# Cross-attention on one core: query weights B11 kept on chip, values loaded by single quads, two copies aside

## The chip, the core and the metric

The kernel runs on one core of a Trainium2 chip. The core has five engines with queues of their own: TensorE (PE, with its weight loads, PEld, shown apart), VectorE (DVE), ScalarE (ACT), GpSimd (POOL) and SyncE (SP), which here issues nearly all DMA transfers. The metric is the device time of one execution in microseconds; lower is better.

## What is computed

Everything is float32. `x` is 8 batches of 256 rows of 1024; `ctx` has the same shape and serves as keys and as values; there are 32 heads of 32 columns.

```python
x = (hidden - mu) * rsqrt(var + 1e-5) * ln_gamma + ln_beta
Q, K, V = split_heads(x @ Wq.T), split_heads(ctx), split_heads(ctx)
scores = einsum('bhsd,bhtd->bhst', Q, K) * 32 ** -0.5
probs = softmax(where(mask, scores, -inf))
attn = einsum('bhst,bhtd->bhsd', probs, V)   # heads joined again
return hidden + attn @ Wout.T
```

## The kernel before

The work is cut into 64 quads of four heads (128 columns): quad n is batch n // 8, column block n % 8. The main loop (L903) has 64 slots, and slot n works on several quads at once: scores of quad n+1 (L479), softmax of quad n+1, values of quad n-2 (L622), a share of the output product of the batch before (L694), and a share of the queries for a later batch. Every engine runs its instructions in the order in which this loop writes them; the schedule is written out by hand, and engines meet through semaphores.

**Softmax and the moves behind it** (softmax_parts, L491). DVE takes the row minimum (L515; queries are made with a negative scale), ACT the exponential (L519), DVE the reciprocal of the sum (L526), POOL the scaling (L528), DVE the transpose in blocks of 32 into `pT` (L534, four per quad). Half of `pT` then lies on the wrong partitions. ACT copies this half aside into `pc` (L540, two copies per quad). SP then issues two moves pT<-pT (L600), then the loads that the slot has in a list `between`, then two moves pT<-pc (L604), which overwrite what the first two moves have read and so wait for their landing. Another list, `ahead`, is issued before the first moves. In slots 0 to 6 and 56 to 61 this tail of a quad is put off to the next slot, behind its first exponentials. `pc` lies in the pool `asp` with three buffers, `pT` in one with three.

**Values** (load_v, L140). One transfer of 512 KB loads the values of two quads, in `between` of every second slot; the pool `vp` has two such buffers.

**Queries.** For batches 0 to 2 the product is made with the whole weights (make_q, L331). From batch 3 on a batch is made with seven products of half size (a Strassen-like scheme) in the order of Q_PRODUCTS, one per slot, from slot 8(b-1)+2 on: 18, 26, 34, 42 and 50 (query_product, L432). Seven weight tiles of 8 KB a partition are needed: four quarters (B11, B12, B21, B22) and sums T1 to T4, which POOL makes in slots 9 to 22 (sum_wq, L385). The tile `wq` holds four of the seven; T3 and then T2 take the place of B12, and T4 that of B11. T1, B11 and T3 are stored to DRAM (keep_wq, L393) and pass in turn through the tile `ring` in each batch (load_ring, L405, halves of 512 KB): T1 three and two slots before the first product, B11 both halves in the slot of the first product, T3 both halves two slots later. The products that read the ring are S1 (first), A11 (third) and S3 (fifth).

**The start.** Slots 0 to 7 also load the output weights `wo` in eight transfers of 512 KB (L173), the last of them in slot 7, and move blocks of the next batch's x (xnT<-xe, L327). The first output product (A11, then A12, of batch 0) begins in slot 9 in the PSUM bank `po` that the second query product of slot 8 has used; ACT empties it in copy_q (L349). ACT's order at that point is: copy pc<-pT of quad 9, the query copies, second copy pc<-pT.

Of the kernel before, what the change touches and what calls it, by code (L numbers as in the profile page):

```python
# [46 lines left out]
F32 = mybir.dt.float32  # L47
# [4 lines left out]
P = 128  # L52
# [7 lines left out]
def xattn_kernel(  # L60
# [12 lines left out]
    B, S, D = x.shape  # L73
    T = mask.shape[2]
    HD = D // HEADS
# [6 lines left out]
    K = 32  # L82
    NA = P // K
    NI = T // (2 * K)
    assert NH == 4 and NS == 2 and NT == 2 and S == 256 and T == 256 and NA == 4
    NEG_SCALE = -1.0 / math.sqrt(HD)
    N = B * NQ

    const = ctx.enter_context(tc.tile_pool(name="const", bufs=1))
# [4 lines left out]
    vp = ctx.enter_context(tc.tile_pool(name="vp", bufs=2))  # L94
    atp = ctx.enter_context(tc.tile_pool(name="atp", bufs=3))
    ep = ctx.enter_context(tc.tile_pool(name="ep", bufs=4))
    ptp = ctx.enter_context(tc.tile_pool(name="ptp", bufs=3))
    asp = ctx.enter_context(tc.tile_pool(name="asp", bufs=3))
    up = ctx.enter_context(tc.tile_pool(name="up", bufs=1))
    sm = ctx.enter_context(tc.tile_pool(name="sm", bufs=8))  # L100
    dram = ctx.enter_context(tc.tile_pool(name="dram", bufs=1, space=bass.MemoryType.DRAM))
# [6 lines left out]
    NK = D // P // 2  # L108
    ring = const.tile([P, NK, NK, P], F32, tag="ring", name="ring")
# [13 lines left out]
    xs, ks, vs, rs = {}, {}, {}, {}  # L123
# [8 lines left out]
    def load_k(n):  # L132

        b, g = divmod(n, NQ)
        ks[n] = kp.tile([P, 2, T], F32, tag="k", name=f"k_{n}")
        nc.sync.dma_start(
            ks[n], kv[b, g // 2, :, : 2 * T].rearrange("p (g t) -> p g t", g=2)
        )

    def load_v(n):  # L140

        b, g = divmod(n, NQ)
        vs[n] = vp.tile([P, NI, 2 * P], F32, tag="v", name=f"v_{n}")
        nc.sync.dma_start(
            vs[n], kv[b, g // 2, :, 2 * T :].rearrange("p (i v) -> p i v", i=NI)
        )

    def load_res(b, s, h):
# [8 lines left out]
    sums_x = const.tile([P, 2, NK, NA, K], F32, tag="sx", name="sx")  # L157
    kept = {
        name: dram.tile([P, NK, NK * P], F32, tag=name, name=f"kept_{name}")
        for name in ("T1", "B11", "T3")  # L160
    }
    wo = const.tile([P, 7, NK, 512], F32, tag="wo", name="wo")
    B11, B21, B22, T1, T2, T3, T4 = range(7)
    B12 = T1

    def load_wq(o):
        nc.sync.dma_start(wq[:, o], wq_[o])
# [36 lines left out]
    for o in range(2, 5):  # L204
        load_wq(o)
    load_k(2)
    load_v(0)
    for o in range(5, 8):
        load_wq(o)

# [148 lines left out]
    def fold(o):  # L359
# [13 lines left out]
    SPLIT = 3  # L373
    SOON, LATE = 0, NK
    W_AT = {"B12": (SOON, 0), "B22": (SOON, NK), "B11": (LATE, 0), "B21": (LATE, NK),
            "T2": (SOON, 0), "T3": (SOON, 0), "T4": (LATE, 0)}

    def weights(name, o):

        if name == "ring":  # L380
            return ring[:, o]
        first, k = W_AT[name]
        return wq[:, first + o, ds(k, NK)]

    def sum_wq(to, o):  # L385

        to, a, b, op = {
            "T1": ("ring", "B12", "B11", ALU.subtract), "T3": ("T3", "B22", "B12", ALU.subtract),
            "T2": ("T2", "T3", "B11", ALU.add), "T4": ("T4", "B21", "T2", ALU.subtract),
        }[to]  # L390
        nc.gpsimd.tensor_tensor(weights(to, o), weights(a, o), weights(b, o), op)
# [13 lines left out]
    def load_ring(name, half):  # L405
# [1 line left out]
        nc.sync.dma_start(ring[:, pair].rearrange("p o c q -> p o (c q)"), kept[name][:, pair])  # L407

    Q_PRODUCTS = (
        ("S1", "ring", True), ("S4", "B22", False), ("A11", "ring", True), ("S2", "T2", False),  # L410
        ("S3", "ring", False), ("A22", "T4", False), ("A12", "B21", True),
    )

# [18 lines left out]
    def query_product(b, p):  # L432
        name, which, begins = Q_PRODUCTS[p]
        if begins:
            pqs[b] = ps_q.tile([P, NK, P], F32, tag="pq", name=f"pq_{b}_{name}")
        x_ = x_part(b, name)
        for o in range(NK):
            w = weights(which, o)
            for c in range(NK):
                nc.tensor.matmul(  # L440
                    pqs[b][:, o, :], w[:, c], x_[:, c], start=begins and o + c == 0,
                    stop=c == NK - 1, skip_group_check=True,
                )
# [40 lines left out]
    def softmax(*args):  # L484
        for _ in softmax_parts(*args):
            pass
# [127 lines left out]
    def values(n):  # L614
        pvs[n] = [
            ps_v.tile([P, 2, NS, K], F32, tag="pv", name=f"pv_{n}_{r}") for r in range(2)
        ]
        pT = pTs.pop(n)
        for i in range(NI):
            for j in range(NH):  # L620
                for r in range(2):
                    nc.tensor.matmul(  # L622
                        pvs[n][r][j * HD : (j + 1) * HD],
                        vs[n - n % 2][ts(r, 2 * K), i, ds(n % 2 * P + j * HD, HD)],
                        pT[ts(r, 2 * K), :, i, j, :, :],
                        start=(i == 0), stop=(i == NI - 1),
                    )

    def copy_at(n):
        b, c = divmod(n, NQ)  # L630
        k, c = divmod(c, NK)
        if c == 0:
            ats[b, k] = atp.tile([P, NK, NS, NA, K], F32, tag="at", name=f"at_{b}_{k}")
        for r, pv in enumerate(pvs.pop(n)):
            nc.scalar.copy(  # L635
                ats[b, k][:, c, :, ts(r, 2), :], pv.rearrange("p a s k -> p s a k")
            )
# [144 lines left out]
    firsts = {NQ * (b - 1) + 2: b for b in range(SPLIT, B)}  # L782
# [55 lines left out]

    away, rings = {n: [] for n in range(N)}, {n: [] for n in range(N)}
    for n, name, half in (  # L840
        (9, "B11", 0), (10, "B11", 1), (15, "T1", 0), (16, "T1", 1), (17, "T3", 0), (19, "T3", 1),
    ):
        away[n].append(partial(keep_wq, name, half))
    for n, b in firsts.items():
        for slots, name in (((n - 3, n - 2), "T1"), ((n, n), "B11"), ((n + 2, n + 2), "T3")):
            if b > SPLIT or name != "T1":
                for half, slot in enumerate(slots):
                    rings[slot].append(partial(load_ring, name, half))
# [35 lines left out]
    for b in range(B - 1):  # L884
        done, ends = 0, b == B - 2
        for i, counts in enumerate(ENDS if ends else STEPS):
            n = NQ * (b + 1) + i
# [15 lines left out]
    for n in range(N):  # L903
        b, i = divmod(n - NQ, NQ)
        new_q = new_qs[n]
        between = []
        if n % 2 and n + 1 < N:
            between.append(partial(load_v, n + 1))
        elif n % 2 == 0 and n + 4 < N:
            between.append(partial(load_k, n + 4))  # L910
        ahead = rings[n]
        if n + 3 in firsts or n + 2 in firsts:
            between, ahead = between + ahead, []
        if b >= 0:
            if b == B - 2 and i - 1 in (5, 6):
                between.append(partial(send, b, *ENDS_TO[i - 1]))
# [24 lines left out]
        if n >= 2:  # L941
            values(n - 2)
# [20 lines left out]
        if n + 1 < N:  # L963
            softmax(n + 1, copies, ahead, between, hooks, fill)
        else:
            copy_at(n - 2)
            for load in between:
                load()
        if b >= 0 and i == 1:
            sum_at(b, "S2", *((slice(NK - 1, NK),) if b == B - 2 else ()))  # L970
# [68 lines left out]
    for c in range(2):  # L1039
        end_steps(to_c11, "A12", B21, (c,), (0,))  # L1040
        end_steps(to_c21, "A22", T4, (c,), (0,))
    values(N - 2)
    copy_at(N - 2)
    end_sum(slice(2, 3), nc.gpsimd)
# [3 lines left out]
    s2t2 = ps_o.tile([P, 512], F32, tag="po", name="po_end_s2")  # L1048
    end_steps(s2t2, "S2", T2, range(2), (0,))
    values(N - 1)  # L1050
    copy_at(N - 1)
    end_sum(slice(3, 4), nc.vector)
# [66 lines left out]
```

## Time and profile before

| what | us |
|---|---|
| median of three runs | 575.7 (574.19 to 576.84) |
| span of the profiled execution, first to last instruction | 577.6 |
| PE busy | 567.7 (98%) |
| DVE, ACT, POOL busy | 458.6, 412.1, 404.7 |
| values, v<-in_kv: 32 transfers of 512 KB, median to landing | 4.2 |
| keys, k<-in_kv: 32 of 256 KB | 3.0 |
| ring: 18 of 512 KB from T1 and T3, 10 from B11 | 5.8 and 5.9 |
| pT<-pT and pT<-pc: 128 each, 128 KB | 2.9 and 4.7 |

In all 117.98 MB were moved by the transfers, at 204 GB/s on average. No time of the profiled execution is given beside its span, so the span stands for it; it is 1.9 us above the median of the timed runs.

How to read the lines further on. A line of the timeline gives start, length, engine, source line, operation, output<-input, and in square brackets the idle time before it with what ended it. "issue" is waiting for which the profile shows no cause. SPq and PEld are the queues of SP and of PE's weight loads. Each float32 matmul of the program stands as two matmuls in the trace. A line of stages gives the stretch, its length, and then for PE, PEld, DVE, ACT and POOL the busy time with the number of instructions; then PE's granted clock, the busy share of the DMA engines and GB/s.

### The profile page before, as it was taken

Reading aid. Unit: us, or ns where it says so; the run is one execution under the profiler, and the core shown is the slowest. Engines: PE = TensorE matmul, PEld = TensorE weight load, DVE = VectorE, ACT = ScalarE, POOL = GpSimd, SP = SyncE. Lnnn points to the kernel's source line nnn. Section 1 sums busy time; section 2 is a strip of 40 time slices with the busy share of each in tenths; the row PEclk is TensorE's granted clock in tenths of the full one; section 3 lists DMA queues with packets and bytes.
Section 4 is the critical chain, followed back from the end, with each engine's and each line's share of the span. In section 5 each row is a group of like instructions: output and inputs, shape, how many; then the busy total and the mean of one; then the engine's idle time right before and its main releaser. Section 6 shows DMA issues by size and latency. Waiting matters only on the chain.

```text
span 577.6 us, 20001 instructions
## 1 busy us (share of the span) xinstructions
PE 567.7 (98%) x7162; PEld 392.2 (68%) x7162; DVE 458.6 (79%) x1695; ACT 412.1 (71%) x1425; POOL 404.7 (70%) x672
## 2 busy tenths in 40 slices
PE   8999998999999999899999999999999999999998
PEld 8788884666667777477776677667766777755444
DVE  6897887687878878678888888888877868879823
ACT  4688886677758857678577976779767866869820
POOL 1788998699896896665657775676656667448780
PEclk9999999999999999999999999999999999999999
DMA  8675778756778667776686767887658865436741
GB/s 312 224 211 184 218 240 209 244 172 196 196 229 271 215 188 219 225 222 202 181 247 181 233 196 201 237 257 217 186 160 254 239 192 147 130 112 182 214 154 74
DMA packets 47475, 117.98 MB, mean 204 GB/s; under 512 B 9104, under 2 KB 9872, under 8 KB 47376
## 3 DMA queue, kind: packets, MB, share of 16 engines
q1 hardware_dynamic: 47088, 116.69, 68.2%
q8 instruction: 57, 0.93, 0.7%
q14 instruction: 42, 0.34, 0.2%
q10 hardware_dynamic: 288, 0.01, 0.0%
HBM read 65.28 MB, written 11.53 MB: 133 GB/s over the span
## 4 chain that ended last, share of the span: by engine, by line
PE 79%; POOL 8%; DVE 6%; issue 2%; DMA 2%; ACT 1%; SPq 0%; DVEq 0%; POOLq 0%; ACTq 0%
PE po_S L694 17%; PE pq_A L440 16%; PE sc L479 10%; PE po_A L694 10%; PE pv L622 9%; PE pq_S L440 6%; POOL e L528 6%; PE pq L340 6%; DVE e L515 3%; PE po_end L761 2%; DVE pT L534 1%; PE po_last L761 1%; POOL wo L183 1%; DMA pT<-pT 1%; ACT e L519 1%
## 5 line engine op out<-in xcount | busy, mean ns | idle before, releaser
L528 POOL TENSOR_SCALAR e<-e,rden 128x256 f32<-128x256 f32 x512 | 237.0, 483 | 131.1 <-DVE rden L526 129.6
L519 ACT ACTIVATE e<-e,mn 128x256 f32<-128x256 f32 x512 | 254.0, 500 | 53.8 <-DVE mn L515 53.8
L534 DVE STREAM_TRANSPOSE pT<-e 128x512 f32<-128x512 f32 x256 | 180.7, 707 | 54.8 <-POOL e L528 43.8
L515 DVE CUSTOM_DVE_ANT_0 e<-sc,mb 128x256 f32<-128x256 f32 x512 | 185.9, 416 | 23.7 <-PE sc L479 23.2
L540 ACT COPY pc<-pT 128x512 f32<-128x512 f32 x128 | 79.0, 617 | 72.0 <-DVE pT L534 43.0
L519 ACT ACTIVATION_READ_ACCUMULATOR e<-e,mn 128x1 f32 x512 | 97.7, 191 | 0.0
L340 PE MATMUL pq<-xnT,wq 128*128 128x256 f32 (+1 forms) x368 | 84.1, 383 | 0.0
L340 PEld LDWEIGHTS pq<-xnT,wq 128*128 128x128 f32 x368 | 68.7, 190 | 14.3 <-issue 3.9
L479 PEld LDWEIGHTS sc<-k,qa 32*128 32x128 f32 x1024 | 46.2, 184 | 42.4 <-issue 20.6
L694 PE MATMUL po_S<-wo,at 128*128 128x512 f32 x152 | 74.5, 607 | 0.3 <-DVE r L736 0.3
L622 PE MATMUL pv<-pT,v 64*32 64x128 f32 x4096 | 74.3, 274 | 0.0
L622 PEld LDWEIGHTS pv<-pT,v 64*32 64x32 f32 x4096 | 56.9, 105 | 25.3 <-issue 11.9
L479 PE MATMUL sc<-k,qa 32*128 32x256 f32 x1024 | 73.6, 400 | 0.1
L694 PE MATMUL po_A<-wo,at 128*128 128x512 f32 x128 | 61.9, 616 | 4.2 <-issue 2.2
L694 PE MATMUL po_S<-wo,s 128*128 128x512 f32 x104 | 50.2, 606 | 0.3 <-DVE r L736 0.3
L515 DVE DVE_READ_ACCUMULATOR2_ANT mn<- 128x1 f32 x512 | 42.6, 83 | 0.0
L694 PEld LDWEIGHTS po_A<-wo,at 128*128 128x128 f32 x128 | 22.6, 190 | 29.2 <-issue 23.4
L526 DVE RECIPROCAL rden<-den 128x2 f32<-128x2 f32 x256 | 37.5, 146 | 5.9 <-ACT e L519 4.6
L440 PEld LDWEIGHTS pq_A<-xnT,wq 128*128 128x128 f32 x320 | 37.3, 192 | 4.8 <-issue 4.1
L694 PEld LDWEIGHTS po_S<-wo,at 128*128 128x128 f32 x152 | 25.6, 190 | 20.8 <-issue 19.3
L440 PE MATMUL pq_A<-xnT,wq 128*128 128x128 f32 x320 | 37.3, 275 | 0.0
L635 ACT COPY at<-pv 128x128 f32<-128x128 f32 x128 | 26.2, 253 | 8.7 <-PE pv L622 8.7
(95 smaller groups left out, 605.3 us busy)
## 6 DMA issues: line engine op xcount, KB each, us to landing
v<-in_kv_dram SPq DMA_DIRECT2D x32, 512.0 KB, 4.2
pT<-pT SPq DMA_DIRECT2D x128, 128.0 KB, 2.9
pT<-pc SPq DMA_DIRECT2D x128, 128.0 KB, 4.7
ring<-kept_T SPq DMA_DIRECT2D x18, 512.0 KB, 5.8
k<-in_kv_dram SPq DMA_DIRECT2D x32, 256.0 KB, 3.0
x<-in_x_dram SPq DMA_DIRECT2D x14, 512.0 KB, 5.5
r<-in_x_dram SPq DMA_DIRECT2D x28, 256.0 KB, 4.5
out_dram<-r SPq DMA_DIRECT2D x28, 256.0 KB, 3.9
```

The lines of the kernel that those rows point to most:

```text
L340: nc.tensor.matmul(pqs[n], wq[:, o, c, :], xnTs[b](c), start=(c == 0), stop=(c == NC - 1),)
L440: nc.tensor.matmul(pqs[b][:, o, :], w[:, c], x_[:, c], start=begins and o + c == 0, stop=c == NK - 1, skip_group_check=True,)
L479: nc.tensor.matmul(scs[n][j][:, s, :], qa[r, n % NQ, ts(s, P)], ks[n - n % 2][r, n % 2, :], start=True, stop=True,)
L515: nc.vector.tensor_tensor_reduce(out=e[:, s, :], in0=pss[j][:, s, :], in1=mbs[n // NQ], scale=1.0, scalar=NO_SCORE, op0=ALU.add, op1=ALU.m ...
L519: nc.scalar.activation(e[:, s, :], e[:, s, :], AF.Exp, bias=mn[:, s : s + 1], scale=-1.0, accum_out=den[:, s : s + 1],)
L526: nc.vector.reciprocal(rden, dens[j])
L528: nc.gpsimd.tensor_scalar(es[j][:, s, :], es[j][:, s, :], rden[:, s : s + 1], 1.0, ALU.mult, ALU.mult,)
L534: nc.vector.transpose(pT[:, :, :, j, :, :].rearrange("p a i s k -> p (a i) s k"), es[j].rearrange("p s (b t) -> p b s t", t=K),)
L540: nc.scalar.copy(pc[:, :, ts(j, 2)], pT[:, 1, :, ts(j, 2)])
L622: nc.tensor.matmul(pvs[n][r][j * HD : (j + 1) * HD], vs[n - n % 2][ts(r, 2 * K), i, ds(n % 2 * P + j * HD, HD)], pT[ts(r, 2 * K), :, i, j, ...
L635: nc.scalar.copy(ats[b, k][:, c, :, ts(r, 2), :], pv.rearrange("p a s k -> p s a k"))
L694: nc.tensor.matmul(po, operand(b, name)[:, c], wo[:, which, c], start=begins and c == 0, stop=c == NK - 1, skip_group_check=not begins,)
```

## The change

T4 gets a tile of its own, `w_t4`, so B11 stays in its place in `wq` for the whole run; product A11 reads it there, and B11 is neither stored to DRAM nor loaded. Room comes from the values, which are loaded by single quads (256 KB) into two buffers of half the size, and from `asp`, which has two buffers instead of three. The values of quads 0 and 1 are loaded at the start, and those of quad n from 2 on in slot n, in `ahead`. T3's halves are loaded in the slot of the first product and the next (in batch 3: two slots later), in `between`; the ring loads no longer go into `ahead`. The host lays the values out so that a quad's part of a partition is one run of 2 KB.

```diff
-    asp = ctx.enter_context(tc.tile_pool(name="asp", bufs=3))
+    asp = ctx.enter_context(tc.tile_pool(name="asp", bufs=2))
...
-        vs[n] = vp.tile([P, NI, 2 * P], F32, tag="v", name=f"v_{n}")
+        vs[n] = vp.tile([P, NI, P], F32, tag="v", name=f"v_{n}")
         nc.sync.dma_start(
-            vs[n], kv[b, g // 2, :, 2 * T :].rearrange("p (i v) -> p i v", i=NI)
+            vs[n],
+            kv[b, g // 2, :, ds(2 * T + n % 2 * NI * P, NI * P)].rearrange("p (i v) -> p i v", i=NI),
         )
...
-        for name in ("T1", "B11", "T3")
+        for name in ("T1", "T3")
     }
+    w_t4 = const.tile([P, NK, NK, P], F32, tag="t4", name="t4")
...
     load_v(0)
+    load_v(1)
...
-            "T2": (SOON, 0), "T3": (SOON, 0), "T4": (LATE, 0)}
+            "T2": (SOON, 0), "T3": (SOON, 0)}
...
+        if name == "T4":
+            return w_t4[:, o]
...
-        ("S1", "ring", True), ("S4", "B22", False), ("A11", "ring", True), ("S2", "T2", False),
+        ("S1", "ring", True), ("S4", "B22", False), ("A11", "B11", True), ("S2", "T2", False),
...
-                        vs[n - n % 2][ts(r, 2 * K), i, ds(n % 2 * P + j * HD, HD)],
+                        vs[n][ts(r, 2 * K), i, ts(j, HD)],
...
-        (9, "B11", 0), (10, "B11", 1), (15, "T1", 0), (16, "T1", 1), (17, "T3", 0), (19, "T3", 1),
+        (15, "T1", 0), (16, "T1", 1), (17, "T3", 0), (19, "T3", 1),
...
-        for slots, name in (((n - 3, n - 2), "T1"), ((n, n), "B11"), ((n + 2, n + 2), "T3")):
+        for slots, name in (
+            ((n - 3, n - 2), "T1"), ((n, n + 2 if b == SPLIT else n + 1), "T3"),
+        ):
...
-        if n % 2 and n + 1 < N:
-            between.append(partial(load_v, n + 1))
-        elif n % 2 == 0 and n + 4 < N:
+        if n % 2 == 0 and n + 4 < N:
             between.append(partial(load_k, n + 4))
-        ahead = rings[n]
-        if n + 3 in firsts or n + 2 in firsts:
-            between, ahead = between + ahead, []
+        ahead = [partial(load_v, n)] if n > 1 else []
+        between += rings[n]
...
-            for load in between:
+            for load in ahead + between:
                 load()
```

More of the change, by code (lines that the diff above doesn't have):

```diff
@@ L1091 @@
     keys = keys.transpose(0, 1, 3, 2, 4).reshape(B, D // 256, P, 2 * T)
-    values = v.reshape(B, T // 64, 64, D // 256, 256).transpose(0, 3, 2, 1, 4)
+    values = v.reshape(B, T // 64, 64, D // 256, 2, P).transpose(0, 3, 2, 4, 1, 5)
     values = np.tile(values.reshape(B, D // 256, 64, 4 * T), (1, 1, 2, 1))
```

## The prediction

> **What bounds the kernel now.** I read the page's first part, then busy time by stage, then the timelines of PE, ACT and SP where PE is not full. TensorE is busy 98% of the span:
>
> ```profile
> PE 567.7 (98%) x7162; PEld 392.2 (68%) x7162; DVE 458.6 (79%) x1695; ACT 412.1 (71%) x1425; POOL 404.7 (70%) x672
> ```
>
> That share alone would not say that PE is the bound, but by stage (length, then busy time of PE, PEld, DVE, ACT, POOL) it does:
>
> ```profile
> 90.00:100.00 10.00, 8.20 (x94) 3.73 (x92) 7.58 (x29) 6.59 (x22) 8.80 (x13) 1.00 0.72 204
> 174.00:240.00 66.00, 66.00 (x852) 46.60 (x854) 54.78 (x200) 50.04 (x175) 53.45 (x86) 1.00 0.77 231
> 240.00:250.00 10.00, 7.81 (x111) 6.35 (x104) 6.84 (x28) 5.26 (x20) 5.24 (x10) 0.83 0.65 196
> 310.00:510.00 200.00, 200.00 (x2705) 141.50 (x2712) 162.65 (x602) 146.99 (x515) 128.47 (x226) 1.00 0.69 200
> ```
>
> From 174 to 240 and from 310 to 510 us PE has no hole. Its blocks also repeat to a few ns: worked out from the starts in the trace, 61 of the 64 blocks of values (L622) take 1.09 us, and all five A11 products read from the ring take 3.57 us, though one engine's transfers fill 0.7 of the time. So ring loads hold up nothing that PE reads, and taking them away frees nothing in these stages. Adding up by how much each PE block exceeds the usual length of its kind gives 9.0 us in the whole span; this is all that a change of transfers could win between PE's first and last block. 5.7 us of it stand in two places.
>
> The first is the start of batch 0's output product (slots 9 and 10):
>
> ```profile
> 88.10 1.15 PE L479 MATMUL sc<-k,qa 32*128 32x256 f32 x16
> 89.49 3.70 PE L694 MATMUL po_A<-wo,at 128*128 128x512 f32 x8 [0.24 <-ACT qa L349]
> 93.12 1.16 PE L622 MATMUL pv<-pT,v 64*32 64x128 f32 x64
> 98.06 1.13 PE L694 MATMUL po_A<-wo,at 128*128 128x512 f32 x2 [1.71 <-DMA wo<-in_woT_dram]
> 99.11 1.15 PE L479 MATMUL sc<-k,qa 32*128 32x256 f32 x16
> 100.19 1.16 PE L622 MATMUL pv<-pT,v 64*32 64x128 f32 x64
> ```
>
> PE waits for the last quarter of the output weights (1.7 us, 2.0 against its usual pace). The second is 241.57 to 247.1 us: 2.19 us without a releaser that the profile shows, then PE at half clock for 3.41 us, 3.8 us lost. A 16 KB instruction fetch was in flight from 241.28 to 242.38; that it caused the hole is a guess.
>
> **Removed.** Ten ring loads of B11 (512 KB, median 5.9 us to landing) and two stores: 6.3 of 118 MB, about 5% of the traffic. Cover: PE at its pace, above. Worth 0 in full stages; at most the 3.8 us hole goes, if it came from traffic. I take 0.5 (12% of 3.8: the twelve are among 98 transfers of 512 KB).
>
> **At no cost.** The order of instructions on PE, ACT, DVE and POOL is the same in both kernels, apart from operands. T4 written to its own tile is the same POOL subtraction (L391, 2.56 us for two). A11 reads wq instead of ring, with the same rows and strides. PE gains 5 extra wait conditions among some 830. ACT gains two conditions on each of 62 copies pc<-pT; that copy usually follows 0.5 to 1.5 us of idle (72 us in all), which hides them. T3's halves go behind the first pair of pT moves, a slot apart, and are read four slots after the first load; they push the second pair (pT<-pc) back by one 512 KB load, some 2 us, and in those slots this pair lands 7 us or more ahead of its reader. Without that cover it would cost 2 us in each of five batches.
>
> **Value loads.** SP issues 32 more transfers of values and 12 fewer others, 20 x 0.57 = 11 us of issuing, against 200 us in which SP waited for work. A quad's load (256 KB) waits for the values of two quads before, on SP, ahead of the pT moves of the next quad. In steady slots that matmul block ends some 6 to 10 us before those moves have data, so nothing is held; the load has a slot and more to land (keys of the same size: median 3.0 us). In the last slot it leaves after the last pT<-pc (554.2 us), lands near 557.5 and is read at 560.4. Tighter is slot 7: quad 7's load goes behind quad 7's pT<-pc (landed 91.04), so it lands at some 92.1 and is read at 93.12. The exception is quad 8, below.
>
> **Two copies aside.** ACT's copy pc<-pT of quad n now waits until pT<-pc of quad n-2 has landed. From the landings in the trace this leaves over 1 us of slack in every slot but two, the first of which is quad 9:
>
> ```profile
> 82.25 1.16 SPq L604 DMA_DIRECT2D pT<-pc  x2
> 92.96 5.58 SPq L327 DMA_DIRECT2D xnT<-xe  x6
> 98.65 0.53 SPq L600 DMA_DIRECT2D pT<-pT  x1
> ```
>
> ```profile
> 88.44 0.62 ACT L540 COPY pc<-pT 128x512 f32<-128x512 f32 x1 [0.92 <-DVE rden L526]
> 88.97 0.83 ACT L349 ACTIVATE qa<-pq,qa 128x256 f32<-128x256 f32 x2
> ```
>
> Quad 7's pair leaves at 82.25 and takes 8.2 us, the longest of its kind, behind keys, x and wo; its second half lands at 91.04. Quad 9's copy starts at 88.44 and would wait 91.04 - 88.44 = 2.6 us. Behind it on ACT stand the two query copies, and PE's A11 at 89.49 already waits for them (0.24). So PE starts 2.6 late. That is the new wait, on the path. It swallows the old one: PE then asks for wo after 98.06 + (2.6 - 1.7) = 98.96, when it has landed (98.02), so 1.7 is given back: **+0.9**.
>
> Then quad 8's values. They were loaded with quad 9's at 84.7; now the load stands behind the six xnT moves, at the place where SP issues at 98.65. At 3.0 us (keys) it lands at 101.7, and PE, 0.9 late, wants it at 101.1: **+0.6**. These 3.0 us are the nearest row; the bounds are 2.8 and 6.4 of the same group. Quad 10's copy moves back with the rest and finds its buffer free. The residual r (DVE waits 3.6 us for it near 102) comes later by one 256 KB load, about 1 us, as PE does.
>
> The sum: 577.6 + 0.9 + 0.6 - 0.5 = 578.6, which is +1.0. The profiled execution stands 1.9 above the median, by about half of the 241 us event. Carried to the median: 575.7 + 1.0 = 576.7. As an estimate, I replayed the queue with transfers at their measured spacing without the slow wo transfer: quad 7's pair then lands near 89.4, the wait is 1.0, and nothing else waits; PE is +1.0 there too. I take **576.5**.
>
> Bounds of the unknown: the ACT wait 0 to 3.1 us; the quad 8 load 0 to 1.5 (landing at 101.7 with PE on its old time), and 4.0 at the group's slowest, 6.4; the old wo wait 1.7 to 2.0 given back or not there; the 241 us event 0 to 3.8; and the clock. On that: the hole of 2.19 us was followed by 3.41 us at half clock (32 matmuls of L440 in 4.38 in place of 3.57 us, two of L694 in 1.66 in place of 0.96: 1.5 us lost), the wait before 98.06 was followed by none. A wait of 2.6 us can go either way, 0 to 1.5.
>
> The Trainium skill ("TensorE: Matmul & The Clock Gate", What's actually happening) has the clock halve after an idle window of some 3.4 us, free-running. By that neither hole should have been followed by half clock, and the new wait would cost no clock; the trace's 2.19 us contradicts the length, so the row decides. By the rule the sum is the same and the top of the range 1.5 lower; by the row the 1.5 stays in it.
>
> **Rivals.**
> 1. Waits change hands (my forecast, 0.5): 575.2 to 578.2.
> 2. The relief decides: quad 7's pair lands before 88.44, wo is early (its queue holds 256 KB less), the 241 us event stays away: 577.6 - 2.0 - 3.8 = 571.8 in its own terms, near 573 against a median that has only part of these losses. For it: the fastest run before, 574.2. Against: wo and the pair share one queue, so what makes one late makes both. 0.25.
> 3. Slower, by ACT held at quad 9: the full 3.1 us there, quad 8's values 1.5 later, half clock 1.5, less 1.7: +4.4, 580.1. It decides once the pair of quad 7 lands after some 91.5. 0.2.
> 4. The pc wait recurs: quad 42 has 1.2 us of slack before (its like in two other batches 2.9 and 3.1), in a slot that all batches from the fourth share. Its cover is that the 512 KB values ahead of that pair move out; if it still lands 1 to 2 us late, four batches pay 4 to 8 us: about 582. 0.05.
>
> That the change does not remove the traffic is excluded: the ten loads and two stores are not in the new SP order.
>
> **Numbers.** 0.5% of 575.7 is 2.9 us, about what a measurement can tell from no change: below 572.8 is faster, above 578.6 slower. Faster: under half of rival 2, 0.11. Slower: most of rivals 3 and 4, 0.22. The rest 0.67. The range 572.6 to 580.3 leaves out the lower end of 2, the upper of 3 and all of 4.
>
> **What would show it.** Right: PE full from 174 to 240 and 310 to 510 us, apart from a possible instruction hole; ACT pc L540 waiting for DMA pT<-pc near 88 us; PE po_A waiting 1 to 3 us for ACT qa L349; no or little wait for wo; PE pv waiting under 1.5 us for v near 101. DMA bytes at 111 to 112 MB. Wrong: PE waits for v in steady slots, ACT waits for pT<-pc in each batch, or PE blocks of one kind that become shorter in full stages.

## The result and the profile after

The changed kernel takes 578.2 us (median of 15 runs, 576.6 to 579.7) against 575.7 of the kernel before (15 runs beside it). That is 2.5 us slower. The ratio is 1.0046, 95% interval 1.0032 to 1.0060: inside the 0.5% that was taken as no change, but close to its edge, and the interval reaches beyond it.

The profiled execution of the changed kernel has a span of 577.7 us and a time of 579.5, so span and time are 1.8 apart. By the same difference the profiled execution of before (span 577.6) took 579.4, which is 3.7 above its median. The two profiles have equal spans, and yet the kernels differ: which part of each profile belongs to every execution has to be settled first.

Stages first, from the profile after (length, busy time of PE, PEld, DVE, ACT, POOL with instructions, PE's granted clock, DMA share, GB/s):

```profile
60.00:90.00 30.00, 30.00 (x416) 24.18 (x400) 25.69 (x101) 23.80 (x86) 27.67 (x42) 1.00 0.75 210
90.00:100.00 10.00, 6.53 (x10) 2.53 (x8) 5.20 (x24) 4.82 (x16) 7.23 (x11) 0.66 0.79 216
174.00:240.00 66.00, 66.00 (x916) 46.93 (x915) 53.64 (x202) 49.41 (x172) 52.72 (x84) 1.00 0.73 208
240.00:250.00 10.00, 10.00 (x127) 7.02 (x123) 8.66 (x32) 6.63 (x26) 6.74 (x12) 1.00 0.75 216
310.00:510.00 200.00, 200.00 (x2728) 141.84 (x2732) 162.65 (x602) 146.69 (x515) 127.69 (x226) 1.00 0.66 184
```

The full stages are full as before in this profile, with less traffic (208 against 231 GB/s, 184 against 200); the second profile of the same kernel, at the end of the experiments, has a hole in one of them. The page's sum of bytes shows that the transfers are gone:

```profile
DMA packets 50101, 111.69 MB, mean 193 GB/s; under 512 B 9425, under 2 KB 10193, under 8 KB 50001
```

The stretch 240 to 250, which held the hole of before, has none. The loss stands in 90 to 100: PE is busy for 1.7 us less than before, and at a clock of 0.66. PE's timeline there:

```profile
88.87 1.15 PE L484 MATMUL sc<-k,qa 32*128 32x256 f32 x16
93.48 6.64 PE L699 MATMUL po_A<-wo,at 128*128 128x512 f32 x8 [3.47 <-ACT qa L352]
100.05 1.16 PE L627 MATMUL pv<-pT,v 64*32 64x128 f32 x64
...
104.99 1.16 PE L627 MATMUL pv<-pT,v 64*32 64x128 f32 x64
```

ACT's at the same place, and two lines of DVE's:

```profile
92.43 0.62 ACT L545 COPY pc<-pT 128x512 f32<-128x512 f32 x1 [4.22 <-DMA pT<-pc]
92.96 0.83 ACT L352 ACTIVATE qa<-pq,qa 128x256 f32<-128x256 f32 x2
93.68 0.62 ACT L545 COPY pc<-pT 128x512 f32<-128x512 f32 x1
```

```profile
87.90 0.69 DVE L229 BATCH_NORM_STATS2 st<-x 128x6 f32<-128x512 f32 x1 [1.47 <-DMA x<-in_x_dram]
...
89.76 0.69 DVE L539 STREAM_TRANSPOSE pT<-e 128x512 f32<-128x512 f32 x1
```

The copy aside of quad 9 waits 4.2 us; the move pT<-pc of quad 7, which landed at 92.33, came last. The query copies stand behind it on ACT; PE's A11 waits 3.5 us for them. But the missing buffer is not all of this wait. The copy also needs the first two transposes of quad 9, and the second of them ended only at 90.45, because DVE had waited 1.47 us for rows of x that a later batch needs. In the profile before, DVE does not wait there, and that transpose ended at 88.40:

```profile
85.86 0.69 DVE L226 BATCH_NORM_STATS2 st<-x 128x6 f32<-128x512 f32 x1
...
87.71 0.69 DVE L534 STREAM_TRANSPOSE pT<-e 128x512 f32<-128x512 f32 x1
```

So the buffer holds ACT from 90.45 to 92.43, for 2.0 us. PE's A11 waits 3.2 us longer than before (3.47 against 0.24): 2.0 us of it by the buffer, some 1.2 by the late x.

Then PE runs at half clock from 92.61 to 99.43, twice 3.41 us, and the eight matmuls that take 3.70 at full clock take 6.64. Neither the wait for wo nor one for quad 8's values is left. Summed over PE's blocks as in the prediction, the excess is 8.6 us against 9.0: 6.5 in slot 9 against 5.8 at the two old places, and 2.1 elsewhere against 3.2.

### The profile page after: what moved, and what is told of

It is laid out like the page before. It is cut to its first block, busy times and chain, and to the rows that moved or that the text cites. A ratio compares the mean times of both kernels' runs of the same rounds, so it can differ in the third digit from the quotient of the medians.

```text
span 577.7 us, 20132 instructions
## 1 busy us (share of the span) xinstructions
PE 569.0 (98%) x7162; PEld 394.2 (68%) x7162; DVE 458.4 (79%) x1695; ACT 411.7 (71%) x1425; POOL 403.3 (70%) x672
## 4 chain that ended last, share of the span: by engine, by line
PE 90%; DVE 3%; POOL 3%; ACT 1%; issue 1%; DMA 1%; SPq 0%; DVEq 0%; ACTq 0%; POOLq 0%
PE po_S L699 19%; PE pq_A L445 16%; PE po_A L699 11%; PE sc L484 11%; PE pv L627 11%; PE pq L343 9%; PE pq_S L445 6%; PE po_end L766 2%; POOL e L533 2%; DVE e L520 1%; DVE pT L539 1%; PE busy L120 1%; PE po_last L766 1%; ACT e L524 1%; DMA x<-in_x_dram 1%
## 5 line engine op out<-in xcount | busy, mean ns | idle before, releaser
L699 PE MATMUL po_A<-wo,at 128*128 128x512 f32 x128 | 63.8, 635 | 3.5 <-ACT qa L352 3.5
```

Of the source, the lines that this page charges most:

```text
L699: nc.tensor.matmul(po, operand(b, name)[:, c], wo[:, which, c], start=begins and c == 0, stop=c == NK - 1, skip_group_check=not begins,)
```

## The experiments

Ratios are to the kernel before, run on the same chip beside them. Its medians were 575.5 (runs of the first four and of the last four kernels) and 576.0 (the others). Since the base differs, two kernels of different groups are compared by their ratios.

**The third copy-aside buffer alone.** The kernel before with one edit:

```diff
-    asp = ctx.enter_context(tc.tile_pool(name="asp", bufs=3))
+    asp = ctx.enter_context(tc.tile_pool(name="asp", bufs=2))
```

> The kernel before with one part of the change alone: two buffers for the copies aside instead of three. Theory A (ACT's copy of quad 9 waits for the pair pT<-pc of quad 7, and the query copies behind it on ACT hold PE's first A11): the wait appears here as well. In the profile of before the pair landed at 91.04 us and the copy started at 88.44, so ACT waits 2 to 4 us, PE 2 to 4 us for ACT qa, PE runs some 3.4 to 6.8 us at half clock after it, and the wait for wo near 98 us is gone: 577 to 579 us, slower than before by 0.3 to 0.6%. Theory B (the loss comes from the moved and split value loads or the moved T3 loads): no wait at quad 9 that costs, 575 to 576.3 us.

577.7 us (573.4 to 581.0), 1.0038 [1.0010, 1.0065]. PE's timeline and the waits of this kernel:

```profile
92.57 5.33 PE L694 MATMUL po_A<-wo,at 128*128 128x512 f32 x8 [2.54 <-ACT qa L349]
```

```profile
ACT pc L540 <- DMA pT<-pc: 3.3, 1, 3.3
```

So this edit alone makes the chain of the changed kernel, half clock included (92.5 to 95.9), and the wait for wo is gone. Here the transposes were ready at 89.22 (DVE waits only 0.18 us for x), and the copy started at 91.52, so the buffer alone holds it for 2.3 us. By the medians this edit gives most of the loss.

The runs of this kernel scatter, and the clock sorts them. One stretch of 3.41 us at half clock lowers the mean granted clock of an execution by 0.003 (3.41 x 0.5 / 577). Five runs with none have a median of 574.8, four with one 578.1, three with two 580.8. So this edit does not cost the same in each execution: against the 575.5 of the kernel before, nothing in the five without half clock, and 2.7 to 5.3 us in the others. The clock does not make these steps alone. By the same figures a stretch costs 1.7 us at most (3.41 x 0.5), and the steps are 3.3 and 2.7; so the clock also marks the executions in which PE waits longer. Nor does the mean tell where a stretch stood: in the profiled execution of this kernel one is at slot 9 and the other follows the hole near 241 us.

The same sorting for the kernels with a part in the dispute (mean granted clock of 0.999 or 1.0, of 0.996 or 0.997, and of 0.993 or 0.994; a dash where there was no such run):

| kernel | no half clock: runs, median us | one stretch | two |
|---|---|---|---|
| before (runs beside the experiments) | 77, 575.8 | - | - |
| after | 4, 577.4 | 8, 578.1 | 3, 579.5 |
| asp alone | 5, 574.8 | 4, 578.1 | 3, 580.8 |
| quad 8's values early (below) | 3, 576.2 | 7, 577.6 | 2, 579.6 |
| unread matmuls in the wait (below) | 12, 577.2 | - | - |

None of 77 runs of before had such a stretch; its profiled execution had one, at 243.67. That stretch, and with it a part of the 3.8 us, is not in the median. The second profiled execution of before (at the end of the experiments) has one too, at another place; why these two executions have one and the 77 have none, no run shows.

**The ACT wait alone taken away.** The changed kernel, with quad 9's copies in two free slots of `ring`:

```diff
+        if n == NQ + 1:
+            pc = ring[:, 2:4].rearrange("p o c q -> p (o c q)")
+            pc = pc.rearrange("p (i h s k) -> p i h s k", i=NI, h=NH, s=NS)
+        else:
+            pc = asp.tile([P, NI, NH, NS, K], F32, tag="pc", name=f"pc_{n}")
```

> The changed kernel, but quad 9's copies aside go into the half of ring that is unused until slot 14, so this one quad has a third buffer. Theory A: ACT's copy near 88 us waits for no DMA, PE's A11 starts within 0.5 us of the end of the scores, no half clock there; a wait for wo of 0 to 1.5 us may come back: 574.5 to 576.5 us, the whole loss of 2.5 us won back. Theory B: the time stays at 577.5 to 578.5 us, as all of the moved loads are still there.

579.8 (578.3 to 580.7), 1.0086 [1.0061, 1.0112]: slower than the changed kernel. A miss, with its reason in PE's and SP's timelines:

```profile
90.50 3.70 PE L703 MATMUL po_A<-wo,at 128*128 128x512 f32 x8 [0.40 <-ACT qa L352]
...
102.83 2.08 PE L631 MATMUL pv<-pT,v 64*32 64x128 f32 x64 [3.25 <-DMA v<-in_kv_dram]
```

```profile
94.84 4.72 SPq L330 DMA_DIRECT2D xnT<-xe  x6
99.66 0.53 SPq L144 DMA_DIRECT2D v<-in_kv_dram  x1
```

A11 starts 3 us earlier, and PE stops at quad 8's values instead: they were issued behind six xnT moves at 99.66 and landed at 102.70. Half clock follows from 103.0 to 106.4. In the changed kernel the same load is as late, and nobody sees it, since PE is already later. All six runs had half clock, four of them twice; why the median lies above that of the changed kernel the one profile (its span 578.0) does not show.

**The query copies ahead of quad 9's first copy aside.** The changed kernel, one step earlier in the two loops that emit these copies:

```diff
-        if n <= NQ:
+        if n <= NQ + 1:
...
-        if n > NQ:
+        if n > NQ + 1:
```

> The changed kernel with the buffers as they are, but on ACT the query copies of slot 8 stand ahead of quad 9's first copy aside (the rule that puts them behind it begins one quad later). ACT still waits some 3 to 5 us for the pair of quad 7, but PE's A11 doesn't stand behind that. Theory A: 574.5 to 576.5 us; ACT pc waits for DMA pT<-pc about 4 us, PE for ACT qa under 0.5 us. Rival C (ACT's wait reaches PE in another way, by the exponentials of quad 10 that stand behind it): PE waits 2 to 4 us later on, 577.5 to 578.5 us. Theory B: 577.5 to 578.5 us with no wait of PE here.

578.2 (577.0 to 579.8), 1.0063 [1.0041, 1.0085]. PE's timeline:

```profile
89.30 3.70 PE L699 MATMUL po_A<-wo,at 128*128 128x512 f32 x8
92.93 1.16 PE L627 MATMUL pv<-pT,v 64*32 64x128 f32 x64
96.37 4.54 PE L699 MATMUL po_A<-wo,at 128*128 128x512 f32 x6 [2.28 <-ACT p L707]
...
102.30 1.25 PE L627 MATMUL pv<-pT,v 64*32 64x128 f32 x64 [0.32 <-DMA v<-in_kv_dram]
```

A11 no longer waits. But ACT still stands at the copy aside until quad 7's pair has landed (91.65; the copy starts at 91.75, after 2.9 us of idle), and now the emptying of `po` (L707) is behind it: the wait moved one block on, 2.28 us with half clock after it.

**The clock by itself.** The changed kernel with 14 matmuls into an unread PSUM tile, ahead of A11 in slot 9:

```diff
+        if n == NQ + 1:
+            warm = ps_v.tile([P, P], F32, tag="pv", name="warm")
+            for _ in range(14):
+                nc.tensor.matmul(
+                    warm, wo[:, B11, 0, :P], wo[:, B11, 0, :P], start=True, stop=True,
+                )
```

> The changed kernel with 14 matmuls more on PE (128x128, about 3.1 us at full clock, into a PSUM bank that nobody reads) just ahead of batch 0's first A11 step in slot 9, where PE would be idle 3.5 us. The wait itself stays. Theory A with the clock as a price of its own (in the profile of the changed kernel PE ran 6.83 us at half clock after the wait, and the eight matmuls of A11 took 3.0 us more than usual): the half clock does not come, 575.2 to 576.8 us. If the wait alone is the price and the half clock costs nothing that counts: 578 to 579.5 us.

577.2 (576.5 to 577.9), 1.0033 [1.0016, 1.0051]. PE's timeline:

```profile
89.79 3.39 PE L940 MATMUL warm<-wo 128*128 128x128 f32 x28
93.02 3.60 PE L699 MATMUL po_A<-wo,at 128*128 128x512 f32 x8
...
102.45 1.25 PE L627 MATMUL pv<-pT,v 64*32 64x128 f32 x64 [0.90 <-DMA v<-in_kv_dram]
```

PE has 3.4 us of work more than in the changed kernel, and the kernel is not slower for it. The added work sits where PE waited anyway, and A11 runs at full clock. No run of this kernel had half clock. So the clock is a price of its own, 6.64 - 3.60 = 3.0 us at A11 in the profile after. Over all runs it is less: 1.1 us by the medians, 0.7 by the two ratios, whose intervals overlap. The median lies between the two ranges that were expected. A part of the gain is lost again a few us later, where PE, now earlier, waits 0.90 us for quad 8's values.

**Both gates taken away.** Quad 9's copies aside in `ring` as above, and quad 8's values loaded into another free slot of it in slot 7, after wo:

```diff
-        vs[n] = vp.tile([P, NI, P], F32, tag="v", name=f"v_{n}")
+        vs[n] = ring[:, 1] if n == NQ else vp.tile([P, NI, P], F32, tag="v", name=f"v_{n}")
...
-        ahead = [partial(load_v, n)] if n > 1 else []
+        ahead = [partial(load_v, n)] if n > 1 and n != NQ else []
...
+            if n == NQ - 1:
+                between.append(partial(load_v, NQ))
```

> The changed kernel with both suspects of slots 9 and 10 out of the way: quad 9's copies aside in the unused half of ring (as in the second run), and quad 8's values in another unused quarter of ring, so that their load can go in slot 7, behind wo and ahead of pT<-pc, in place of slot 8 behind the six xnT moves. Theory A2 (two waits lie one behind the other, ACT for the pair of quad 7 and PE for quad 8's values; taking one away brings out the other, and both must go): neither wait in the profile, wo costs 0.5 to 2 us, no half clock: 573.5 to 575.5 us. Theory B (the rest of the moved and split loads costs the time): 577 us or more with PE waits elsewhere.

576.6 (575.6 to 581.3), 1.0015 [0.9996, 1.0034]: most of the loss is won back, though a microsecond less than expected. No wait for pT<-pc or for values is left in the profile, and there is no half clock (one of the 12 runs, the one of 581.3, had two stretches). What is left in slots 9 and 10 are two waits of a microsecond on PE:

```profile
90.48 3.70 PE L703 MATMUL po_A<-wo,at 128*128 128x512 f32 x8 [1.17 <-ACT qa L352]
...
105.98 1.52 PE L703 MATMUL po_S<-wo,s 128*128 128x512 f32 x3 [1.11 <-DVE r L745]
```

The first is the late x again: DVE waits 1.06 us for it ahead of quad 9's transposes, the copy aside waits for them, and the query copies stand behind the copy. DVE has this wait in all nine profiles of the changed kernel and its variants (0.26 to 1.80 us), and at most 0.26 us in the five of the kernel before and its variants. No run takes it away by itself.

**Quad 8's values early, copies as in the change** (the last diff alone):

> The changed kernel with quad 8's values loaded early alone (in an unused quarter of ring, in slot 7); the copies aside as in the changed kernel. Theory A2: ACT still waits 3 to 5 us for the pair of quad 7 and PE 2.5 to 4 us for ACT qa; the values are there earlier but nobody waited for them: 577 to 578.7 us, as the changed kernel. If the values' load were the whole cause: 574 to 576 us.

577.5 (575.4 to 579.8), 1.0029 [1.0010, 1.0047]. The wait of the copies is there as in the changed kernel. PE's timeline and waits:

```profile
93.41 5.40 PE L699 MATMUL po_A<-wo,at 128*128 128x512 f32 x8 [3.81 <-ACT qa L352]
```

```profile
ACT pc L545 <- DMA pT<-pc: 4.5, 1, 4.5
```

**Both, and wo first in slot 7** (order wo, quad 8's values, x):

```diff
-                between.append(partial(load_v, NQ))
+                between[:0] = [partial(load_wo, which, pair), partial(load_v, NQ)]
+            else:
+                between.append(partial(load_wo, which, pair))
```

> As the run with both suspects taken away, and in slot 7 the last quarter of the output weights is loaded first, then quad 8's values, then x. Theory A2: also the wait for wo (0.8 to 1.7 us in earlier profiles) goes: 572.5 to 574.5 us, below the kernel before. If the loads only change places in a full queue: PE or DVE waits 1 to 2 us for x or for the pair of quad 8 instead, 574 to 576 us.

577.0 (575.5 to 579.1), 1.0019 [1.0000, 1.0037]; above both ranges, the first by 2.5 us and the second by 1.0. The wait for wo is gone, but in the profile PE waits 1.3 us for the query copies (DVE 1.18 for x before that), 1.1 in two places for the residual r and, in a later batch near 311 us, 0.75 for a move pT<-pT. So the loads changed places, as the second forecast had it.

**wo first, in the kernel before:**

```diff
-            between.append(partial(load_wo, which, pair))
+            between.insert(0 if n == NQ - 1 else len(between), partial(load_wo, which, pair))
```

> The kernel before with one edit: in slot 7 the last quarter of the output weights is loaded ahead of the values and of x. In the profile of before PE lost 2.0 us to this load. If that wait is there in most executions: 573 to 574.5 us; if it is an accident of the one that was profiled: 575 to 576 us. The event near 241 us (2 to 2.5 us without a releaser, then half clock) is expected to show again, as nothing near it changes.

575.8 (573.9 to 576.6), 0.9988 [0.9972, 1.0004]. The wait of 1.7 us for wo is gone from the profile, and the median moves by less than can be told. Later waits take part of its place (0.77 for the residual near 105). The hole near 241 us shows again, 1.42 us long and without half clock.

**Values by single quads in the kernel before.** Two buffers of half size, each load ahead of the slot's first moves; B11 still passes through `ring`, `asp` keeps three buffers, the ring loads keep their places:

```diff
-        if n % 2 and n + 1 < N:
-            between.append(partial(load_v, n + 1))
-        elif n % 2 == 0 and n + 4 < N:
+        if n % 2 == 0 and n + 4 < N:
...
+        if n > 1:
+            ahead = [partial(load_v, n)] + ahead
...
-            for load in between:
+            for load in ahead + between:
```

> The kernel before with another part of the change alone: values by single quads into two small buffers, loaded in the slot that frees the buffer (three buffers for the copies aside and B11 through the ring as before). Theory A2: ACT waits for no pT<-pc at quad 9, but quad 8's values, behind six xnT moves on SP, land near 102 us and PE waits 2 to 3.5 us for them, with half clock after it: 577 to 579.5 us. If this part costs nothing by itself: 575 to 576.3 us.

589.4 (five runs, 582.0 to 589.7; a sixth took 591.4), 1.0213 [1.0173, 1.0252], far more than either theory expected. The profiled execution was the fastest of the six, so it shows only a part. In it a full stage is no longer full (PE lacks 3.5 us of 200; the most in another profile is 1.0, in the second one of the changed kernel):

```profile
310.00:510.00 200.00, 196.45 (x2655) 140.00 (x2652) 160.13 (x597) 146.30 (x514) 125.15 (x223) 1.00 0.72 203
```

PE waits in later batches too, where values, a half of a ring load and the moves leave within a few us of one another (values 306.78, moves from 307.25, ring 309.07). Two of these places, with slot 10 ahead of them, in PE's timeline:

```profile
101.34 1.42 PE L624 MATMUL pv<-pT,v 64*32 64x128 f32 x64 [2.48 <-ACT e L521]
...
311.30 1.26 PE L624 MATMUL pv<-pT,v 64*32 64x128 f32 x64 [1.16 <-DMA pT<-pT]
...
381.71 1.26 PE L624 MATMUL pv<-pT,v 64*32 64x128 f32 x64 [1.36 <-ACT pc L542]
```

The wait at 101.34 stands where the one for quad 8's values was expected (they were issued at 98.10, behind the six xnT moves). The trace puts it down to ACT, though ACT had finished that quad's exponentials long before, and shows no landing for these values; so that PE waited for them is likely and not shown.

From 240 to 250 PE is busy all 10 us: the hole of before is not there, although B11's loads are.

**The repaired version.** Both gates away, the query copies first, and batch 0's first residual loaded in slot 5:

```diff
-            if i < 4:
+            if i < 4 and n != NQ:
...
+            if n == 5:
+                between.append(partial(load_res, 0, 0, 0))
```

> The run with both suspects taken away, and two edits more: the query copies of slot 8 stand ahead of quad 9's first copy aside on ACT, and batch 0's first residual is loaded in slot 5 in place of slot 8. In the profile of that run PE waited 1.2 us for ACT qa near 90 us and 1.1 us for DVE, which waited for the residual, near 106 us. Theory A2: both go, 574 to 575.3 us, a little below the kernel before. If the time is set elsewhere: 576 to 577 us as that run.

575.2 (574.3 to 576.6), 0.9998 [0.9986, 1.0009]. The stretch is nearly clean, with one wait of 0.71 us for ACT (L711) and no half clock. By the ratios it is 2.8 us below the changed kernel, and it is level with before. The last two edits act together here, so the 1.0 us that they gain on the run with both gates away is not divided between them.

**Each kernel once more, for a second profile.**

> The kernel before once more, unchanged, for a second profile. If the event near 241 us (2 to 2.5 us without a releaser, then half clock) belongs to this kernel's timing, it shows again, as it did with two buffers for the copies aside; if it is an accident, PE is full there. The wait for wo near 97 us: 0 to 2 us.

> The changed kernel once more, unchanged, for a second profile: ACT pc waits 3 to 5 us for DMA pT<-pc near 88 us, PE 2.5 to 4 us for ACT qa, half clock for one or two stretches of 3.41 us, and no event near 241 us.

Before took 577.6 in this execution. The wait for wo is there again (1.73 us), and this time half clock follows it, from 100.3 to 103.7; so does the hole, shorter and without half clock:

```profile
243.62 1.02 PE L694 MATMUL po_A<-wo,at 128*128 128x512 f32 x2 [1.09 <-issue]
```

After took 579.5, with the known wait and one stretch at half clock, and nothing at 241. But PE also waits in a stage that was full in the first profile, for a half of T1 in `ring`:

```profile
92.68 5.40 PE L699 MATMUL po_A<-wo,at 128*128 128x512 f32 x8 [3.15 <-ACT qa L352]
...
315.19 2.05 PE L445 MATMUL pq_S<-sx,ring 128*128 128x128 f32 x16 [0.85 <-DMA ring<-kept_T]
```

With the slower blocks around it this place costs some 1.6 us against the first profile, which is why the two spans are equal (577.7) although the first has a second stretch at half clock.

## Why the prediction was right, and where its numbers were off

**The place and the mechanism were right.** ACT held at quad 9 by quad 7's pair, the query copies behind it, PE behind them: the trace after shows it, the asp edit alone makes it, and with both gates open the loss is gone within the interval. The swallowed wait for wo, the bytes and the sign of the sum came as worked out, and so did the full stages, but for the 1.6 us in the second profile. The class came out with little to spare: the median is 0.4 us under the 578.6 from which the prediction would have called it slower, and the rise of 0.8 that it took was a third of the 2.5 measured. Terms that were missing and a term that was not paid partly cancel, and that is luck.

**The wait for the buffer was sized about right; a second wait in front of it was missing.** 2.6 us were expected, with an upper bound of 3.1. The asp edit alone has 2.3 (from 89.22 to 91.52), the changed kernel 2.0 in one profile and 2.1 in the other. But ACT stood still for 4.2 us and A11 waited 3.2 us longer than before, because x also came late to DVE, and so the transposes came late to the copy. The prediction took the order of loads to cost nothing here. In the profile after, SP issued that x at 83.43 in place of 81.23 and quad 7's pair at 84.46 in place of 82.25: the pair before went out at 75.38 in place of 73.57, then came a values load that was not there before (0.53), then the six xnT moves in 4.29 in place of 3.76. So x landed at 87.88 in place of 85.83, and the pair at 92.33 in place of 91.04.

**The clock was left out of the sum.** It was in the range with 0 to 1.5. In the profile after it is 3.0 of the 6.5 us lost in slot 9. Over all runs it is the smaller part: 11 of 15 had half clock, and the four that had none still took 577.4, 1.7 us more than before. The forecast that it could go either way held; that it would cost 1.5 at most did not, since two stretches can follow one another over the same product. The prediction weighed a rule of the Trainium skill here ("TensorE: Matmul & The Clock Gate", What's actually happening): half clock after an idle window of some 3.4 us. In slots 9 and 10 and at 241, every hole on PE of 2.2 to 3.8 us was followed by it in the profiles (nine of them), one of 1.73 too, and another of 1.71 was not; the stretches last 3.41 us or twice that, which agrees with the window length that the page states.

The traces also show what tells 1.73 from 1.71. Wherever a profile has more than one start of half clock, the starts lie whole multiples of 3.413 us apart (92.61 and 577.30, the second behind PE's last matmul, in the profile after: 142 of them; 92.46 and 246.06 with the asp edit alone: 45); a wait on PE does not shift them. Cut into windows on this grid, PE was idle for 1.73 to 3.28 us of each of the ten windows at whose end half clock began before PE's last matmul, and for at most 1.42 us of any other. The wait of 1.71 us for wo in the profile before straddles a window's end at 96.90, with 0.55 us on one side and 1.16 on the other. So a window need not be idle as a whole. Where the limit lies between 1.42 and 1.73 no run shows; half a window is 1.71.

**Quad 8's values (+0.6) were real and hidden.** The load landed at 103.23 and PE, later than forecast, wanted it at 104.99. Without the first wait it costs 3.25 us of PE. The working found both gates, but added them up as if each were seen; of two gates in line on one engine only the later one shows, and the other is a lower limit on what a repair can win.

**The relief (-0.5) was too small for the pair of profiles, and its reason fell.** The hole at 241 is in all four profiles of the kernel before, or of it with one small edit (2.19, 1.09, 2.42 and 1.42 us), and in none of the changed kernel or its variants. But it is also absent from the kernel with single-quad values, which still moves B11. So the traffic of B11 does not make it by itself, and whether it plays a part at all is not shown. What made it stays open: the single-quad loads and the instruction stream itself, which is different in each of these kernels, could both have moved it.

**The base was an unusual execution.** By span + 1.8 us the profiled execution of before (579.4) is above each of the 77 timed runs (572.2 to 578.7), and it has a half clock that none of those has. In the profiles new losses (6.5) and old ones (5.8) nearly cancel, which is why the spans agree. In the timed runs the half clock at 241 is not there to be won, and giving back the 1.7 us for wo was counted at full value, though removing that wait in the kernel before moved its median by 0.7 us, with 1.6 as the end of the interval. The prediction had put only about half of the 241 event on the profile alone. So the step "carried to the median" failed by more than the sum did: for the two spans +1.0 was forecast and +0.1 measured, for the medians +0.8 and +2.5.

**The rivals.** Rival 3's condition was met (the pair landed after 91.5) and its place was the right one; its 580.1 is near what the changed kernel takes when both stretches of half clock come (579.5, three runs), but by other terms: it had quad 8's values 1.5 us later, which were not paid, and one stretch where there were two. The median lies just at the upper edge of rival 1's own range (575.2 to 578.2). Rival 2 fell: fewer bytes brought nothing where PE was already full. Rival 4 did not occur: of ACT's copies aside, one waits for pT<-pc in the whole trace.

**What stays open.** How much of the loss is due to the late x, since no run moves that load alone. Where the 1.7 us go in the four runs without half clock, of which no trace was kept. Most of the 14 us by which single-quad values slow the kernel before: the half clock was there in all six runs, but runs with one stretch each lie 7 us apart (582.0 and 589.4), so it does not explain them. That the changed kernel is spared this, with no B11 loads and with the ring loads moved, is shown; which of the two spares it was not tried.

## What to carry to other kernels

A buffer that is taken away for room became a wait here at the one place where its transfer is slowest, which is the start, where all first loads share a queue. The in-order engine behind that wait then decides who pays. When an engine waits for several things, the profile names the one that came last; look when the others came before giving the whole wait to it. When one gate is found, look for the next one behind it before pricing a repair: here, by the ratios, opening one alone won 1.0 us (values, within the noise) or lost 2.3 (copies), and opening both won back 1.8. Before taking a sum from one profile to a median, compare its time and its granted clock with those of the timed runs.

## What the runs showed of the hardware

- Half clock came after single holes on PE from 1.7 to 3.8 us; holes of 1.1 to 1.4 us and one of 1.7 were followed by none. Its starts lie on a grid of 3.413 us in each trace, and it began at the end of each window with 1.73 us or more of idle PE (ten of ten) and of none with 1.42 or less.
- Filling such a wait with 3.4 us of unread matmuls kept the clock in all 12 runs and cost nothing: the median is 1.1 us lower than without them (0.7 by the ratios, within the noise).
- Traffic fell by 5% and the full stages did not become shorter; the same bytes of values in twice as many transfers, with smaller buffers and without that relief, cost 2.1%.
- The hole at 241 stood in four of four profiles of before or near it, without a releaser, and in none of the ten others.
